# The last 20 rows of adj on four row groups of TensorE, one for each column block, in five products with adj

## The chip, the cores and the metric

The kernel runs on one core of a Trainium2 chip. The metric is device time in microseconds (us) for one execution; the time of a kernel is the median of several runs. One further execution was recorded by the hardware profiler, and all views of the profile are of that one.

Engines are named as in the profile: PE is TensorE's matmul stream and PEld its weight loads, DVE is VectorE, ACT is ScalarE, POOL is GpSimd, SP is the engine whose queue issues most DMAs. "L255" is line 255 of the kernel before.

## The reference, cut to what matters

Four graph layers on 2708 nodes with 128 features each. Every layer normalizes, and every layer multiplies by the same 2708x2708 matrix adj at least once:

```python
h = relu(layernorm(x))
x = x + L0(h, adj)     # z = leaky(d*(adj @ (d*h)) @ W1 + b1); S = exp(-dist(z)/2), top 4 a row
                       # d2*((S + adj) @ (d2*h)) @ W2 + b2
h = relu(layernorm(x))
x = x + L1(h, adj)     # attention: num = adj @ exp(leaky(r_i + c_j)); H = adj @ (att @ h W)
h = relu(layernorm(x))
x = x + L2(h, adj)     # h @ W_self + (adj @ h / deg) @ W_neigh
h = relu(layernorm(x))
x = x + L3(h, adj)     # relu(adj @ h @ K + b)
```

All data are float32. The products that this case is about are adj times a 2708x128 matrix: two in layer 0, and one each in layers 1, 2 and 3.

## The kernel before

adj is handed in transposed, as `adjT`. The 2708 rows of `adjT` are cut into T = 22 **chunks** of 128 rows; the last one (`i = T - 1 = 21`) has only TAIL = 20 rows. The 2708 columns are cut into six **column blocks** `KBS`: five of 512 and one of 148. The node dimension is also grouped by four chunks into six `GROUPS`, which coincide with the column blocks.

A product is made by `aggregate(y, done, more, kept)`. Its right-hand side `y` lies in SBUF as `[128, 22, 128]` (node in chunk, chunk, feature). For each column block `b` there is one PSUM bank `acc(b)`. `product(i, b)` is one float32 matmul: stationary `y[:w, i, :]`, moving `chunk(i)[:w, block b]`, summed into `out[b]` over all 22 chunks. In the profile each float32 matmul is two records on PE and two weight loads on PEld, under L255.

The loop over chunks has two parts:

- For `i` below `last`, chunk by chunk: all six blocks of chunk `i` are multiplied, while later chunks are loaded through the rotating pool `big` (4 buffers). After every second chunk one of the resident chunks is fetched.
- For `i` from `last` to 21 the chunks stay in SBUF under names `res17` to `res21` (5 of them, for the two products of layer 0) or `res16` to `res21` (6, for the three later products). This is the **tail**, and it goes block by block: for block `b` all remaining chunks, and then `done(b - 1, out)`, which takes the finished block before it out of PSUM and works on.

So in the tail the 20-row chunk comes once in each of the six blocks, as the last matmul of that block. The resident chunks are loaded once for the two products of layer 0 (in the earlier stage that sums the rows of adj on PE, L341), and once for the last three (during the product with `attended`).

The five products and what runs after each block:

| product | right side | `done` | made by |
|---|---|---|---|
| first | `y1` | `to_z` (L390) | `scale_nodes`, L372 |
| second | `y2` | `done_l0` (L653) | L498 to L505, ACT and DVE |
| third | `attended` | `to_h2` (L1181) | `attend` (L1154), called from `node_product` through `ahead` |
| fourth | `h2` | `to_h3` (L1204) | `layernorm_relu` in `to_h2` |
| fifth | `h3` | `to_out` (L1229) | `layernorm_relu` in `to_h3` |

In the second product there is also a stream of 88 indirect DMAs from POOL (L524, `add_near`), four for each chunk of nodes: each gathers rows of `y2` from its copy `ydr` in DRAM, and DVE adds them to `xs` (L530). Those for chunks 0 to 14 are emitted before the product, those for chunks 15 to 21 within `done_l0` and after it. They have 24 buffers.

A scheduler orders the instructions of an engine by the order of the program and by when it thinks they are ready. What is wrapped in `pin(...)` keeps its order among the pinned ones. All loads of chunks are pinned, on SP's queue. The matmuls of `aggregate` are not.

The lines that the change touches most:

Of the kernel before, what the change touches and what calls it, by code (L numbers as in the profile page):

```python
# [18 lines left out]
P = 128  # L19
# [6 lines left out]
def kernel(  # L26
# [18 lines left out]
    nc = tc.nc  # L45
    N, D = x.shape
    assert D == P
    T = -(-N // P)
    TAIL = N - (T - 1) * P
    KBS = [(k0, min(512, N - k0)) for k0 in range(0, N, 512)]  # L50
    NKB = len(KBS)
# [4 lines left out]
    def width(t):  # L56
        return TAIL if t == T - 1 else P
# [88 lines left out]
    def evacuate(dst, src):  # L146
        turn[0] ^= 1
        if turn[0]:
            nc.vector.tensor_copy(dst, src)
        else:  # L150
            nc.scalar.copy(dst, src)

    def pin(ins):

        return tc.keep_in_program_order(ins)

    def acc(b):
        return ps_a.tile([P, 512], F32, name=f"acc{b}")
# [4 lines left out]
    def layernorm_relu(dst, g):  # L163

        t0, t1 = GROUPS[g]
        n = t1 - t0
        st = small.tile([P, 4, 6], F32, name="ln_st")
        mv = small.tile([P, 4, 2], F32, name="ln_mv")
        rs = small.tile([P, 4], F32, name="ln_rs")
        for t in range(t0, t1):  # L170
            nc.vector.bn_stats(st[:, t - t0, :], xs[:, t, :])
            nc.vector.bn_aggr(mv[:, t - t0, :], st[:, t - t0, :])
        root = nc.scalar.activation(rs[:, :n], mv[:, :n, 1], AF.Sqrt, bias=ln_eps)
        nc.vector.reciprocal(rs[:, :n], rs[:, :n])
        nm = small.tile([P, 4], F32, name="ln_nm")
        nc.vector.scalar_tensor_tensor(
            nm[:, :n], mv[:, :n, 0], -1.0, rs[:, :n], op0=ALU.mult, op1=ALU.mult
        )
        for t in range(t0, t1):
            o = t - t0  # L180
            nc.scalar.activation(
                dst[:, t, :],
                xs[:, t, :],
                AF.Relu,
                scale=rs[:, o : o + 1],
                bias=nm[:, o : o + 1],
            )
        return root

    def scale_nodes(dst, src, v, t0, t1):  # L190
        nc.vector.tensor_tensor(
            dst[:, t0:t1, :],
            src[:, t0:t1, :],
            v[:, t0:t1, None].to_broadcast([P, t1 - t0, D]),
            ALU.mult,
        )
# [8 lines left out]
    def transposed(dst, src, g, copy=evacuate):  # L205

        t0, t1 = GROUPS[g]
        p = ps_s.tile([P, 512], F32, name="ps")
        for t in range(t0, t1):
            o = (t - t0) * P  # L210
            nc.tensor.transpose(
                p[:, o : o + width(t)], src[: width(t), t, :], ident[: width(t), : width(t)]
            )
        copy(dst[:, span(g)], p[:, : span(g).stop - span(g).start])

    def node_product(srcT, w, g, use, behind=False):

        t0, t1 = GROUPS[g]
        p = ps_s.tile([P, 4, P], F32, name="ps")
        for t in range(t0, t1):  # L220
            if w is None:
                nc.tensor.transpose(p[: width(t), t - t0, :], srcT[:, cols(t)], ident)  # L222
            else:
                mm = nc.tensor.matmul(  # L224
                    p[: width(t), t - t0, :], srcT[:, cols(t)], w, start=True, stop=True
                )
                if behind and t == t0:
                    pin(mm)
        for t in range(t0, t1):
            use(t, p[: width(t), t - t0, :])  # L230
# [4 lines left out]
    def chunk(i):  # L235
        if i in resident:
            return resident[i]
        if i >= T - pools["n"]:
            c = resident[i] = pools["res"].tile([P, N + 1], F32, name=f"res{i}")
        else:  # L240
            c = big.tile([P, N + 1], F32, name="chunk", tag="big")
        pin(nc.sync.dma_start(c[: width(i), :N], adjT[i * P : i * P + width(i), :]))
        return c

    def aggregate(y, done, more=None, kept=0):

        out = [acc(b) for b in range(NKB)]
        last = T - pools["n"]  # L250

        def product(i, b):
            k0, n = KBS[b]
            w = width(i)
            nc.tensor.matmul(  # L255
                out[b][:, :n],
                y[:w, i, :],
                chunk(i)[:w, k0 : k0 + n],
                start=(i == 0),
                stop=(i == T - 1),  # L260
            )

        for i in range(last):
            if more is not None:
                more(i)
            resident[i] = chunk(i)
            for b in range(NKB):
                product(i, b)
            if i < last - kept:
                del resident[i]  # L270
            if i % 2 and last + i // 2 < T:
                chunk(last + i // 2)
        if more is not None:
            for i in range(last, T):
                more(i)
        for b in range(NKB):
            for i in range(last, T):
                product(i, b)
            if b:
                done(b - 1, out)  # L280
        done(NKB - 1, out)

    NG = len(GROUPS)
# [14 lines left out]
    y1 = lay.tile([P, T, D], F32, name="y1", tag="Y")  # L298
# [35 lines left out]
    for i in range(T):  # L334
        c = chunk(i)
        w = width(i)
        if 3 <= i < 3 + 3 * NG:
            weighted((i - 3) // 3, i % 3)
        for b, (k0, n) in enumerate(KBS):
            g = 32 * (b % 4)  # L340
# [5 lines left out]
                stop=(i == T - 1),  # L346
            )
    sum_rows = lay.tile([P, 1024], F32, name="sum_rows", tag="U")
    for half, p0, p1 in ((0, 0, 128), (1, 0, 32 * (NKB - 5)), (1, 32 * (NKB - 5), 32 * (NKB - 4))):
        n = KBS[4 * half + p0 // 32][1]  # L350
# [3 lines left out]
    for b, (t0, t1) in enumerate(GROUPS):  # L354
        j = b % 4
        for t in range(t0, t1):
# [6 lines left out]
                stop=True,  # L363
# [7 lines left out]
    nc.gpsimd.tensor_tensor(xs, xs, b2[:, None, :].to_broadcast([P, T, D]), ALU.add)  # L371
    for t0, t1 in GROUPS:  # L372
        scale_nodes(y1, y1, dinv, t0, t1)
    uT = lay.tile([P, N], F32, name="u1T", tag="U")
    z = lay.tile([P, T, D], F32, name="z", tag="Z")
    zT = lay.tile([P, N], F32, name="zT", tag="T")
# [13 lines left out]
    def to_z(g, s1):  # L390
# [24 lines left out]
        evacuate(sq_rows[:, span(g)], p[:3, : span(g).stop - span(g).start])  # L415

    aggregate(y1, to_z)


# [23 lines left out]
    for t in range(T):  # L443
        w = width(t)
# [49 lines left out]
    y2 = lay.tile([P, T, D], F32, name="y2", tag="Y")  # L494
# [25 lines left out]
    def add_near(t, late=False):  # L520
        w = width(t)
        for k in range(TOPK):
            g = res.tile([P, D], F32, name="gath", bufs=24)
            nc.gpsimd.indirect_dma_start(  # L524
                out=g[:w, :],
                out_offset=None,
                in_=ydr[:, :],
                in_offset=bass.IndirectOffsetOnAxis(ap=near_u[:w, t, k : k + 1], axis=0),
            )
            term = nc.vector.scalar_tensor_tensor(  # L530
                xs[:w, t, :],
                g[:w, :],
                simd[:w, t, k : k + 1],
                xs[:w, t, :],
                op0=ALU.mult,
                op1=ALU.add,
            )
            if late and k == 0:
                pin(term)
# [127 lines left out]

    for t in range(15):
        add_near(t)
    aggregate(y2, done_l0, kept=4)  # L670
    transposed(hT, h1, NG - 2, nc.scalar.copy)
    column_terms(NG - 3)
    for t in range(GROUPS[-1][0], T):
# [295 lines left out]
    for t0, t1 in GROUPS:  # L969
        p = acc(1 + t0 // 4 % 5)  # L970
        for t in range(t0, t1):
# [6 lines left out]
                stop=True,  # L978
# [171 lines left out]
    attended = lay.tile([P, T, D], F32, name="attended", tag="Y")  # L1150
# [3 lines left out]
    def attend(t, p):  # L1154
        w = width(t)
        nc.vector.tensor_scalar(attended[:w, t, :], p, wk[:w, t : t + 1], None, op0=ALU.mult)

    def ahead(step, lead):


        def more(i):
            if i == 0:
                for g in range(min(lead + 1, NG)):
                    step(g)
            elif i % 4 == 0 and i // 4 + lead < NG:
                step(i // 4 + lead)

        return more
# [5 lines left out]
    h2 = lay.tile([P, T, D], F32, name="h2", tag="H")  # L1174
# [6 lines left out]
    def to_h2(g, s3):  # L1181
        k0, n = KBS[g]
        evacuate(u3T[:, k0 : k0 + n], s3[g][:, :n])
        node_product(u3T, None, g, add_x)
        layernorm_relu(h2, g)

    aggregate(attended, to_h2, ahead(lambda g: node_product(yT, None, g, attend), 1))

    def own(i):
# [6 lines left out]
    h3 = lay.tile([P, T, D], F32, name="h3", tag="Y")  # L1196
# [7 lines left out]
    def to_h3(g, s4):  # L1204
        k0, n = KBS[g]
        evacuate(u4T[:, k0 : k0 + n], s4[g][:, :n])
        node_product(u4T, wn, g, add_l2)
        layernorm_relu(h3, g)

    aggregate(h2, to_h3, own)  # L1210
    u5T = lay.tile([P, N], F32, name="u5T", tag="Z")

# [66 lines left out]
```

## Time and profile before

| | us |
|---|---|
| median of 3 runs | 1230.08 |
| lowest, highest | 1226.93, 1233.35 |
| the profiled execution's own time | 1316.51 |
| its span, first to last instruction | 1314.5 |
| PE busy (3637 matmul records) | 1094.3, 83% |
| DVE busy | 564.0, 43% |
| ACT busy | 408.5, 31% |
| POOL busy | 229.7, 17% |
| data moved by DMA | 297.31 MB, mean 226 GB/s |
| mean granted TensorE clock | 0.894 |

The five products lie, in us from the start of the span, at about 95 to 203, 350 to 545, 981 to 1086, 1086 to 1202 and 1202 to 1310. The profiled execution is 86 us longer than the median of the runs, so a stage of it has to be read with the clock that was granted in it (the row PEclk of the page, or the clock of a window).

In a group line the columns are: line, engine, operation, output<-inputs, partitions of the operands, shape, count | busy us, mean ns of one | idle time of the engine before them and what ended it. In a timeline line: start us, duration us, engine, line, operation, count, and in brackets the idle time before it and its releaser.

### The profile page before, as it was taken

What the parts mean: (1) busy time and instruction counts of PE and PEld (TensorE: products, weight loads), DVE (VectorE), ACT (ScalarE), POOL (GpSimd) and SP (SyncE); (2) the same over time, 40 slices, a digit from 0 to 9 for tenths busy, and PEclk for the clock granted to TensorE, in tenths of its full rate; (3) what the DMA queues carried; (4) which work ended last, traced back from release to release, by engine and by line L of the source; (5) the groups of instructions that cost most, each with busy time, mean ns of one, the idle gap of its engine ahead of it and who ended that gap; (6) DMA issues with size and microseconds to landing.
All of it is one profiled execution on the core that took longest, in us unless ns stands there. A gap on an engine that the chain in (4) does not pass through costs nothing.

```text
span 1314.5 us, 10207 instructions
## 1 busy us (share of the span) xinstructions
PE 1094.3 (83%) x3637; PEld 516.1 (39%) x3637; DVE 564.0 (43%) x1172; ACT 408.5 (31%) x643; POOL 229.7 (17%) x188
## 2 busy tenths in 40 slices
PE   4979999999673379897777771687899999999998
PEld 1334444444231134463433330233344445545444
DVE  2020026999722001782466564899960021113003
ACT  3100014444400001474566643677830021003000
POOL 1100000000077700034111103577400000000000
PEclk7989999999895569777899885798879999999999
DMA  8997700000562261255899998999939926752831
GB/s 316 425 383 268 282 0 1 1 0 0 193 245 95 94 249 55 86 241 227 227 395 376 359 374 328 422 425 423 351 127 417 354 81 224 268 185 80 302 125 43
DMA packets 39506, 297.31 MB, mean 226 GB/s; under 512 B 6749, under 2 KB 10680, under 8 KB 13116
## 3 DMA queue, kind: packets, MB, share of 16 engines
q1 hardware_dynamic: 23806, 201.04, 39.9%
q0 software_dynamic: 13216, 93.62, 18.9%
q10 hardware_dynamic: 2434, 2.01, 0.6%
q8 instruction: 29, 0.48, 0.1%
q14 instruction: 21, 0.17, 0.0%
HBM read 264.46 MB, written 32.87 MB: 226 GB/s over the span
## 4 chain that ended last, share of the span: by engine, by line
PE 57%; DMA 18%; DVE 11%; issue 10%; POOL 3%; ACT 1%; another core or an unknown queue 0%; SPq 0%; POOLq 0%; DVEq 0%; ACTq 0%
PE acc L255 37%; DMA mov<-in_adj_dram,src_u 8%; PE acc L448 8%; DVE hi L1116 4%; DVE hi L1104 4%; DMA chunk<-in_adj_dram 3%; DMA hi<-table,hi_u 2%; POOL gath L524 2%; PE acc L454 2%; DMA res<-in_adj_dram 2%; PE ps L341 1%; PE ps L224 1%; PE acc L1126 1%; DMA xs<-in_x_dram 1%; PE ps L222 1%
## 5 line engine op out<-in xcount | busy, mean ns | idle before, releaser
L255 PE MATMUL acc<-chunk,y 128*128 128x512 f32 (+1 forms) x408 | 178.8, 588 | 72.7 <-issue 60.1
L1126 PE MATMUL acc<-hi,xw 128*128 128x512 f32 (+2 forms) x264 | 120.9, 618 | 61.5 <-DVE hi L1116 61.5
L524 POOL DMA_INDIRECT gath<-ydr,near_u x88 | 83.4, 948 | 407.9 <-DMA ydr<-y 321.3
L255 PE MATMUL acc<-chunk,h 128*128 128x512 f32 (+1 forms) x384 | 148.0, 542 | 0.0
L255 PEld LDWEIGHTS acc<-chunk,y 128*128 128x128 f32 x408 | 79.0, 204 | 172.4 <-issue 160.6
L1021 PE MATMUL acc<-mov,wt 128*128 128x512 f32 (+1 forms) x264 | 115.2, 588 | 35.8 <-DMA mov<-in_adj_dram,src_u 35.7
L448 PE MATMUL acc<-zT 128*128 128x512 f32 (+2 forms) x264 | 107.7, 552 | 0.0
L1126 PEld LDWEIGHTS acc<-hi,xw 128*128 128x128 f32 (+1 forms) x264 | 54.3, 214 | 127.9 <-DVE hi L1116 64.6
L1025 DVE COPY mov<-acc 2x512 f32<-2x512 f32 (+1 forms) x126 | 74.3, 611 | 63.8 <-PE acc L1021 62.2
L255 PEld LDWEIGHTS acc<-chunk,h 128*128 128x128 f32 x384 | 68.8, 190 | 74.1 <-issue 74.1
L1021 PEld LDWEIGHTS acc<-mov,wt 128*128 128x128 f32 x264 | 51.0, 204 | 96.1 <-issue 69.9
L457 ACT COPY strip<-acc 128x512 f32<-128x512 f32 (+2 forms) x132 | 60.5, 557 | 71.4 <-issue 58.5
L255 PE MATMUL acc<-chunk,attended 128*128 128x512 f32 x192 | 73.5, 545 | 0.0
L448 PEld LDWEIGHTS acc<-zT 128*128 128x128 f32 (+1 forms) x264 | 46.6, 186 | 56.3 <-issue 35.5
L1026 ACT COPY knots<-acc 128x512 f32<-128x512 f32 x88 | 50.5, 586 | 57.4 <-DVE mov L1025 45.2
L1058 POOL DMA_INDIRECT lo<-table,lo_u x22 | 56.1, 2548 | 67.4 <-DVE hi L1104 31.6
L1104 DVE SCALAR_TENSOR_TENSOR hi<-lo,lam,hi 128x2708 f32<-128x2708 f32 (+4 forms) x25 | 67.2, 2697 | 1.0
L1116 DVE SCALAR_TENSOR_TENSOR hi<-row_all,inv_s,hi 128x2708 f32<-128x2708 f32 (+4 forms) x25 | 67.0, 2693 | 0.0
L1108 ACT ACTIVATE hi<-hi,lam 128x2708 f32<-128x2708 f32 (+4 forms) x25 | 56.7, 2280 | 32.3 <-issue 23.2
L459 DVE MAX8 top_v<-strip 128x8 f32<-128x2708 f32 (+1 forms) x22 | 64.7, 2966 | 0.5 <-ACT strip L457 0.4
L461 DVE FIND_INDEX8 top_i<-top_v,strip 128x8 uint32<-128x2708 f32 x20 | 59.2, 2973 | 0.0
L255 PE MATMUL acc<-res,h 128*128 128x512 f32 (+1 forms) x144 | 58.9, 551 | 0.0
(267 smaller groups left out, 1167.8 us busy)
## 6 DMA issues: line engine op xcount, KB each, us to landing
chunk<-in_adj_dram SPq DMA_DIRECT2D x110, 1354.0 KB
table<-knots SPq DMA_DIRECT2D x20, 1354.5 KB
res<-in_adj_dram SPq DMA_DIRECT2D x9, 1354.0 KB
ydr<-y SPq DMA_DIRECT2D x2, 704.0 KB
gath<-ydr,near_u POOLq DMA_INDIRECT x88
chunkY<-in_adj_dram SPq DMA_DIRECT2D x1, 1354.0 KB
chunkU<-in_adj_dram SPq DMA_DIRECT2D x1, 1354.0 KB
table<-knots SPq DMA_DIRECT2D x1, 1333.3 KB
```

The lines of the kernel that those rows point to most:

```text
L255: nc.tensor.matmul(out[b][:, :n], y[:w, i, :], chunk(i)[:w, k0 : k0 + n], start=(i == 0), stop=(i == T - 1),)
L448: mm = nc.tensor.matmul(zz[b][:w, :n], zT[:, cols(t)], zT[:, k0 : k0 + n], start=True, stop=False)
L457: nc.scalar.copy(s[:w, k0 : k0 + n], zz[b][:w, :n])
L459: nc.vector.max(top_v[:w, t, :], s[:w, :])
L461: nc.vector.max_index(top_i[:w, t, :], top_v[:w, t, :], s[:w, :])
L524: nc.gpsimd.indirect_dma_start(out=g[:w, :], out_offset=None, in_=ydr[:, :], in_offset=bass.IndirectOffsetOnAxis(ap=near_u[:w, t, k : k + ...
L1021: nc.tensor.matmul(p[:, :n], wt[:, t, :], moving[t][:, k0 : k0 + n], start=True, stop=True)
L1025: nc.vector.tensor_copy(moving[t + 1][:2, k0 : k0 + n], p[:2, :n])
L1104: nc.vector.scalar_tensor_tensor(num, lo[:w, c], kap, num, op0=ALU.mult, op1=ALU.add)
L1108: nc.scalar.activation(num, num, AF.Ln, scale=sc)
L1116: nc.vector.scalar_tensor_tensor(att[:w, c], row_all[:w, c], inv_s[:w, t : t + 1], att[:w, c], op0=ALU.max, op1=ALU.mult,)
L1126: nc.tensor.matmul(py[b][:, :n], xw[:w, t, :], att[:w, k0 : k0 + n], start=(t == 0), stop=(t == T - 1),)
```

## The change

Chunk 21 is loaded four times, to partitions 0, 32, 64 and 96. Likewise the 20 rows `y[:20, 21, :]` are copied by three small DMAs (`spread`) to partitions 32, 64 and 96, on SP's queue for `y2` and on POOL's for the other four. The six matmuls of chunk 21 use the row group `32 * (b % 4)`, and stand together, ahead of the other resident chunks instead of behind them in each block. The last chunk that closes a sum is now 20.

```diff
--- before.py
+++ after.py
@@ chunk
-        pin(nc.sync.dma_start(c[: width(i), :N], adjT[i * P : i * P + width(i), :]))
+        for g in range(4 if i == T - 1 else 1):
+            pin(
+                nc.sync.dma_start(
+                    c[32 * g : 32 * g + width(i), :N], adjT[i * P : i * P + width(i), :]
+                )
+            )
         return c
 
+    def spread(y, queue):
+
+        for g in range(1, 4):
+            queue.dma_start(y[32 * g : 32 * g + TAIL, T - 1, :], y[:TAIL, T - 1, :])
+
@@ aggregate
         def product(i, b):
             k0, n = KBS[b]
-            w = width(i)
+            r = slice(32 * (b % 4), 32 * (b % 4) + TAIL) if i == T - 1 else slice(0, P)
             nc.tensor.matmul(
                 out[b][:, :n],
-                y[:w, i, :],
-                chunk(i)[:w, k0 : k0 + n],
+                y[r, i, :],
+                chunk(i)[r, k0 : k0 + n],
                 start=(i == 0),
-                stop=(i == T - 1),
+                stop=(i == T - 2),
             )
...
         for b in range(NKB):
-            for i in range(last, T):
+            product(T - 1, b)
+        for b in range(NKB):
+            for i in range(last, T - 1):
                 product(i, b)
             if b:
                 done(b - 1, out)
@@ after scale_nodes of y1
+    spread(y1, nc.gpsimd)
@@
-    aggregate(y2, done_l0, kept=4)
+    aggregate(y2, done_l0, lambda i: spread(y2, nc.sync) if i == 4 else None, kept=4)
@@ attend
         nc.vector.tensor_scalar(attended[:w, t, :], p, wk[:w, t : t + 1], None, op0=ALU.mult)
+        if t == T - 1:
+            spread(attended, nc.gpsimd)
@@ to_h2
         layernorm_relu(h2, g)
+        if g == NG - 1:
+            spread(h2, nc.gpsimd)
@@ to_h3
         layernorm_relu(h3, g)
+        if g == NG - 1:
+            spread(h3, nc.gpsimd)
```

## The prediction

> **What bounds the kernel now.** I first asked for each engine's busy time in the stretches of the five products, since the page's shares mix stages.
>
> ```profile
> core 0: us, PE busy (x) PEld busy (x) DVE busy (x) ACT busy (x) POOL busy (x), PEclk, DMA share, GB/s
> 174.00:203.00 29.00, 29.00 (x101) 13.21 (x100) 12.02 (x38) 6.52 (x29) 0.00 (x0) 1.00 0.00 0
> 385.00:476.00 91.00, 31.29 (x36) 9.76 (x35) 14.37 (x41) 0.00 (x0) 59.19 (x63) 0.52 0.29 92
> 510.00:545.00 35.00, 34.87 (x125) 16.45 (x123) 18.79 (x83) 14.04 (x33) 3.62 (x4) 1.00 0.07 22
> 981.00:1054.00 73.00, 73.00 (x192) 34.35 (x192) 0.89 (x4) 0.00 (x0) 0.00 (x0) 0.99 0.97 389
> 1054.00:1086.00 32.00, 32.00 (x98) 14.51 (x97) 10.94 (x57) 8.57 (x19) 0.00 (x0) 1.00 0.14 53
> 1167.00:1202.00 35.00, 35.00 (x120) 17.22 (x118) 12.64 (x60) 7.58 (x19) 0.00 (x0) 1.00 0.13 49
> ```
>
> PE is busy all the time in the loops and in the tails (174 to 203, 510 to 545, 1054 to 1086, 1167 to 1202), and DVE at most 54% of a tail. So what leaves PE in a tail comes off the end, unless a chain behind it is close. One stretch is of another kind: from 385 to 476 the granted clock is 0.52 and PE does 36 records in 91 us. The second product's loop takes 350.2 to 510.0, 159.8 us; seventeen chunks at 4.54 us (below) are 77.2. **82.6 us of the profiled execution are this stretch**: 1316.5 - 82.6 = 1233.9, within the runs shown (1226.9 to 1233.4). I count gains against that and subtract them from the median.
>
> Next, what a 20-row matmul costs, from the weight loads around one in the third product's tail, in order of time:
>
> ```profile
> 1057.13 0.19 PEld L255 LDWEIGHTS acc<-res,attended 128*128 128x128 f32 x1 [0.24 <-issue]
> 1057.56 0.19 PEld L255 LDWEIGHTS acc<-res,attended 128*128 128x128 f32 x1 [0.24 <-issue]
> 1058.51 0.29 PEld L255 LDWEIGHTS acc<-res,attended 20*128 20x128 f32 x2 [0.76 <-issue]
> 1059.56 0.30 PEld L255 LDWEIGHTS acc<-res,attended 128*128 128x128 f32 x2 [0.76 <-issue]
> 1060.09 0.19 PEld L255 LDWEIGHTS acc<-res,attended 128*128 128x128 f32 x1 [0.24 <-issue]
> ```
>
> Among 128-row matmuls a load comes every 0.43 us, so a 512-column float32 matmul (two records) takes 0.858, the 148-column one 0.25, and a chunk 5 x 0.858 + 0.25 = 4.54. From the load at 1057.56 to that at 1060.09 there are five steps: 5 x 0.43 = 2.15, but 2.53 passed. The gaps of 0.76 say where: the first load of the 20-row matmul, and the first after it, were not made ahead; each waited for the matmul before it. **A visit to the 20-row form costs 0.39 us beside its 0.86.**
>
> Last, how PE runs matmuls on separate strips of the array. The row sums (L341) do, on four column strips; below it is one chunk there, and then one block of the fourth product's tail:
>
> ```profile
> 47.68 1.90 PE L341 MATMUL ps<-chunk,ones 128*32 128x512 f32 x12 [0.74 <-DMA chunk<-in_adj_dram]
> ...
> 1179.18 5.51 PE L255 MATMUL acc<-res,h 128*128 128x512 f32 x12
> ```
>
> Twelve records both, but 1.90 us against 5.51. Six float32 matmuls of the same widths went as two rounds: four strips side by side, then two.
>
> [...]
>
> **The change part by part.**
>
> Removed, in each product: six visits. Five of 512 columns: 0.858 + 0.39 = 1.25 each; where transposes or small matmuls follow instead of L255 the way out is 0.05 cheaper (starts of records), mostly so. The last: 0.25 + 0.39. Sum 5 x 1.25 + 0.64 - 0.25 = 6.6 us.
>
> Added, in each product: one visit with all six. Row group 0 does block 0 and then block 4: 1.72 us; group 1 does 1 and 5 within that. With one way in and out: 1.72 + 0.39 = 2.1. No row shows four row groups at 512 columns, so bounds: below, 2.0[...]; with no overlap 10 x 0.43 + 0.25 + 0.39 = 4.9. I take 2.1, since the strips of L341 came out as two full rounds. **Net 4.5 us a product, 22.5 for five.**
>
> Moved: chunk 21's matmuls go ahead of the tail, so its load and `y`'s last rows must be there some 25 us earlier. For `y1`, `h2`, `h3` the copies follow the last `layernorm_relu` or `scale_nodes`, 70 us or more ahead of the tail. For `attended`, `attend(21)` stands at i = 20 in the program's order, but all 22 L1156 are done at 981.9, before the loop. For `y2` the copies wait for `ydr`'s stores, done when POOL's gathers begin at 358. POOL copies: four products, three issues of about 1 us (the indirect ones take 0.95), landing some 2.4 us later as the gathers do; POOL is idle there, and nothing queues behind but what comes tens of us later. SP copies: three issues of 0.33 us, ahead of chunk loads that wait for buffers anyway. Nothing, as long as the scheduler keeps them early; if `attend(21)` fell to the tail, PE would wait about 6 us (transposes, DVE, issue, landing) once.
>
> Added loads: chunk 21 four times instead of once, twice in the kernel. Its load signals from 11 queues where full ones signal from 16[...]; full chunks land 3.24 us apart when queued, and I take four 20-row loads as one of these[...], 2.4 us more. SP issues six more, 0.35 us each. In the row-sum stage, which waits for DMA, the first copy alone is needed at 86.8 and the others come behind it; the first product's chunks, landing at 89.8, 93.0, 96.3 and 99.5, are due at 95.0 and every 4.54 us after: 2.4 us later still in time (the first by 2.8). In the third product the DMA share is 0.97. Completions in the trace show chunk 12, the one behind chunk 21, landing at 1031.8 and needed at 1035.4: a margin of 3.6 against 2.4. Nothing, up to 1 us.
>
> Who is late next? First product: the chain of `to_z` (DVE 3.5 us a block: the 12.0 above fall in the 20 us from 183, at 5.9 a block) against PE's new block of 4.7, with the steps taking turns on both: I take off 0.5. Second: the gathers. POOL issues one every 1.25 us from 358.0:
>
> ```profile
> 358.02 1.12 POOL L524 DMA_INDIRECT gath<-ydr,near_u  x1 [321.25 <-DMA ydr<-y]
> ...
> 462.15 0.94 POOL L524 DMA_INDIRECT gath<-ydr,near_u  x1 [0.30 <-issue]
> ```
>
> At full clock the tail would begin at 427, and DVE would use those for chunk 19 (the 80th lands at about 459.6) at 464.1 minus what is saved by then, 4: no margin left. I take off 1. Fourth and fifth: DVE has room, PE goes on at once (the fourth) or the last block's chain only shifts (the fifth).
>
> Sum: 22.5 - 0.5 - 1 = 21 us. 1230.1 - 21 = **1209 us**.
>
> **The rivals.**
>
> *The rows don't run side by side*, since the scheduler separates the six, or row groups are served in turn. Then a product saves 6.6 - 4.9 = 1.7: 8.5 us, 1221.5. For it: no row shows row groups at this width. Against: L341. With separate visits the gain falls to nothing.
>
> *The tails are not worth their PE time.* If the gathers hold the second product and `to_z` the first, three products remain, 13.5 us; less 1 for chunk 12: 1217. For it: the margin of 0 us and the short block above. Against: DVE is at 41% in the first tail.
>
> *Slower: the granted clock.* The stretch at 0.52 cost 82.6 us and sits within a product's loop, PE dense, DMA at 0.8 just before. If packed matmuls, or tails with fewer gaps, bring such a stretch into the timed runs, all falls at once: at half clock PE needs 1 us more for each us of work, so 21 us of matmul time in it make the gain zero, and a stretch like that seen gives 1209 + 83 = 1292. Against: nothing in the change raises the work in the loops, where it occurred.
>
> **How the numbers follow.** A measurement of this kernel tells about 0.5% (6 us) from no change. The forecast 0.67; tails not worth their time 0.15, still faster; rows in turn 0.08, of which 0.05 faster; no packing or an offsetting stall 0.04, same; clock 0.06, slower. Faster 0.87, same 0.07, slower 0.06. The range: below, 22.5 us from the fastest run shown (1226.9) is 1204, and 1 us for a cheaper visit: 1203. Above it takes in both faster rivals and their spread: 1223.
>
> **What would show it.** One group of 20-row matmuls ahead of each tail, its twelve records within about 2.1 us, two rounds with four starts close together; every block of the tails shorter by 1.2 us; third to fifth product each shorter by 4.5, with the strip stage (L448) starting 4 earlier after the first. Wrong: the twelve records 0.43 us apart; PE idle before the group, released by DMA of a copy; PE idle at chunk 12 of the third product; DVE's L530 released by `gath` in the second tail and the stage behind it no earlier.

## The result, and the profile after

| | before | after |
|---|---|---|
| median of 20 runs, us | 1231.11 (1226.34 to 1236.05) | 1220.99 (1213.77 to 1229.95) |
| ratio after to before | | 0.9929, 95% interval 0.9913 to 0.9946 |
| profiled execution's own time, span, us | 1316.51, 1314.5 | 1218.29, 1216.2 |

So the change is worth about 9 us (0.71% of 1231; the interval gives 6.6 to 10.7), where 21 were forecast. The group of six matmuls came out as predicted. Less than half of its worth reached the end.

The profile before had a long slow stretch in the second product (granted clock 0.52). For the comparison by stages I use a second profile of the kernel before, taken with the experiments, which has none (span 1228.2). A stage goes from the first matmul of `aggregate` in a product (or the first of the totals, L832) to the next such start, in us:

| stage | before | after | difference | predicted |
|---|---|---|---|---|
| start and row sums, to the first product | 96.2 | 97.6 | +1.4 | 0 |
| first product and strips, to the second | 255.9 | 255.3 | -0.6 | -4.0 |
| second product, to the totals | 138.1 | 133.7 | -4.4 | -3.5 |
| totals, table, attention, to the third | 404.0 | 401.4 | -2.6 | 0 |
| third product, to the fourth | 105.4 | 109.3 | +3.9 | -4.5 |
| fourth and fifth, to the last matmul of `aggregate` | 222.0 | 212.6 | -9.4 | -9.0 |
| the rest | 6.6 | 6.3 | -0.3 | 0 |

The fourth stage holds no edit. Over ten profiles of this study without the slow stretch it ran from 399.8 to 409.4, in no order that follows the edits, so its -2.6 says nothing. The two stages that stand out are the first and the third product.

First the windows over PE's parts of the products after, in answer to those of before (columns as there):

```profile
core 0: us, PE busy (x) PEld busy (x) DVE busy (x) ACT busy (x) POOL busy (x), PEclk, DMA share, GB/s
178.00:203.00 25.00, 25.00 (x96) 12.32 (x95) 10.04 (x30) 6.04 (x29) 0.00 (x0) 1.00 0.00 0
888.00:970.00 82.00, 76.88 (x194) 35.83 (x192) 1.19 (x5) 0.00 (x0) 1.62 (x3) 0.96 0.96 357
970.00:996.00 26.00, 26.00 (x85) 12.61 (x85) 9.33 (x47) 8.17 (x18) 0.00 (x0) 1.00 0.18 63
```

The loop of the third product (888 to 970) now has 5.1 us in which PE does nothing; before it had none. The first tail (178 to 203) still shows PE busy all the time, and yet nothing was gained there; that column misled me, as shown below.

The weight loads around the group of six, third product, in order of time:

```profile
969.68 0.19 PEld L267 LDWEIGHTS acc<-chunk,attended 128*128 128x128 f32 x1 [0.24 <-issue]
970.02 0.31 PEld L267 LDWEIGHTS acc<-res,attended 20*128 20x128 f32 x8 [0.15 <-issue]
970.55 0.19 PEld L267 LDWEIGHTS acc<-res,attended 20*128 20x128 f32 x2 [0.23 <-issue]
970.98 0.19 PEld L267 LDWEIGHTS acc<-res,attended 20*128 20x128 f32 x2 [0.24 <-issue]
971.93 0.30 PEld L267 LDWEIGHTS acc<-res,attended 128*128 128x128 f32 x2 [0.75 <-issue]
```

Twelve loads, of which eight go at once: two rounds, as forecast. From 970.02 to the first 128-row load at 971.93 it is 1.91 us. The step behind that is 0.53 in place of 0.43, and on PE the first 20-row matmul starts 0.22 behind the 148-column one ahead of it, in place of 0.13. So the visit costs 1.91 + 0.10 + 0.09 = 2.1, the forecast. In the first product the first four starts lie within 20 ns.

The third product in the timeline of PE:

```profile
888.04 51.98 PE L267 MATMUL acc<-chunk,attended 128*128 128x512 f32 x132
942.32 6.51 PE L267 MATMUL acc<-chunk,attended 128*128 128x512 f32 x12 [2.29 <-DMA chunk<-in_adj_dram]
951.65 18.44 PE L267 MATMUL acc<-chunk,attended 128*128 128x512 f32 x48 [2.83 <-DMA chunk<-in_adj_dram]
...
980.62 0.60 PE L222 MATMUL ps<-ident,u3T 128*128 128x128 f32 x4
981.05 4.46 PE L267 MATMUL acc<-res,attended 128*128 128x512 f32 x10
985.35 0.60 PE L222 MATMUL ps<-ident,u3T 128*128 128x128 f32 x4
```

The tail is right: a block takes 985.35 - 980.62 = 4.73 us, against 1071.03 - 1065.10 = 5.93 before:

```profile
1065.10 0.66 PE L222 MATMUL ps<-ident,u3T 128*128 128x128 f32 x4
...
1071.03 0.66 PE L222 MATMUL ps<-ident,u3T 128*128 128x128 f32 x4
```

But chunk 11 comes 2.29 us late and chunk 12 another 2.83, and the 12 records between them take 6.51 us, where the 48 behind them take 18.44: the mean clock granted between 938 and 956 is 0.91. The chunk that was late first had been issued *ahead* of the four loads of chunk 21. What moved meanwhile, in the DMA view of 932 to 948, 40 slices of 0.4 us (first row: busy tenths of the 16 engines):

```profile
DMA  9999959969997959979979979896979998999999
GB/s 433 433 433 433 379 108 190 217 135 217 217 217 135 271 81 162 162 108 163 162 108 135 163 108 163 163 190 190 325 271 406 406 406 298 433 379 406 379 406 379
```

For some 10 us the engines stay almost as busy as before and move 81 to 271 GB/s in place of 406 to 433. The busy share hides it; the second row shows it.

### The profile page after: what moved, and what is told of

It is laid out like the page before. It is cut to its first block, busy times and chain, and to the rows that moved or that the text cites. A ratio compares the mean times of both kernels' runs of the same rounds, so it can differ in the third digit from the quotient of the medians.

```text
span 1216.2 us, 10253 instructions
## 1 busy us (share of the span) xinstructions
PE 1054.7 (87%) x3637; PEld 507.0 (42%) x3637; DVE 563.8 (46%) x1172; ACT 407.5 (34%) x643; POOL 237.0 (19%) x200
## 4 chain that ended last, share of the span: by engine, by line
PE 53%; DVE 20%; DMA 19%; issue 6%; POOL 1%; ACT 1%; SPq 0%; POOLq 0%; DVEq 0%; ACTq 0%
PE acc L267 40%; DMA mov<-in_adj_dram,src_u 7%; DVE top_v L474 5%; DMA chunk<-in_adj_dram 5%; DVE top_i L476 5%; DVE hi L1131 4%; DVE hi L1119 4%; DMA hi<-table,hi_u 2%; DMA res<-in_adj_dram 2%; PE ps L847 2%; PE acc L1036 2%; PE acc L1141 1%; PE ps L224 1%; DMA xs<-in_x_dram 1%; PE ps L355 1%
## 5 line engine op out<-in xcount | busy, mean ns | idle before, releaser
L267 PE MATMUL acc<-chunk,y 128*128 128x512 f32 (+1 forms) x408 | 159.3, 554 | 12.8 <-DVE y L518 10.7
L267 PE MATMUL acc<-chunk,h 128*128 128x512 f32 (+1 forms) x384 | 148.0, 542 | 0.0
L1036 PE MATMUL acc<-mov,wt 128*128 128x512 f32 (+1 forms) x264 | 119.7, 608 | 28.7 <-DMA mov<-in_adj_dram,src_u 28.7
L267 PEld LDWEIGHTS acc<-chunk,y 128*128 128x128 f32 x408 | 75.0, 194 | 97.1 <-issue 85.6
L463 PE MATMUL acc<-zT 128*128 128x512 f32 (+2 forms) x264 | 108.2, 552 | 1.5 <-ACT strip L472 1.1
L267 PEld LDWEIGHTS acc<-chunk,h 128*128 128x128 f32 x384 | 68.8, 190 | 74.1 <-issue 74.1
L267 PE MATMUL acc<-chunk,attended 128*128 128x512 f32 x192 | 76.9, 563 | 5.1 <-DMA chunk<-in_adj_dram 5.1
L463 PEld LDWEIGHTS acc<-zT 128*128 128x128 f32 (+1 forms) x264 | 46.4, 185 | 57.3 <-issue 34.1
L545 DVE SCALAR_TENSOR_TENSOR xs<-gath,simd,xs 128x128 f32<-128x128 f32 (+1 forms) x88 | 30.6, 351 | 59.9 <-DMA gath<-ydr,near_u 59.2
```

Source lines behind the costliest of these rows:

```text
L267: nc.tensor.matmul(out[b][:, :n], y[r, i, :], chunk(i)[r, k0 : k0 + n], start=(i == 0), stop=(i == T - 2),)
L463: mm = nc.tensor.matmul(zz[b][:w, :n], zT[:, cols(t)], zT[:, k0 : k0 + n], start=True, stop=False)
L1036: nc.tensor.matmul(p[:, :n], wt[:, t, :], moving[t][:, k0 : k0 + n], start=True, stop=True)
```

## The experiments

Each is timed beside the kernel before on one chip; 95% intervals in brackets.

**The kernel before again** (no edit).

> The kernel before, once more, for a profile in which no long stretch is throttled. Theory (the five tails gain unequally): its second product's loop runs at full clock in about 77 us, the first tail's blocks take about 6.2 us each by the chain of to_z as in the profile already shown, the third product takes 103.8 us, the fourth and fifth together 221.7 us. Rival (the stages differ from profile to profile by several us whatever the kernel): these move by more than 1.5 us.

Span 1228.2, one run at 1230.2 us. Its stages are the "before" column above: loop of the second product without the slow stretch, the third 105.4 by this table's ends, fourth and fifth 222.0. Between the two profiles of before the first product with the strips repeats within 0.7 us (255.2 and 255.9) and the third product within 0.3 (105.1 and 105.4).

**Copies of chunk 21 loaded later.**

```diff
-        for g in range(4 if i == T - 1 else 1): (four loads)
+        (one load in chunk(); the other three in copies())
@@ aggregate, loop over chunks
             resident[i] = chunk(i)
+            if i == late:
+                copies()
-    aggregate(y1, to_z)
+    aggregate(y1, to_z, late=8)
(and late=15 in the third product)
```

> The changed kernel with the three extra copies of chunk 21 loaded later: in the first product after chunk 8's load, in the third after chunk 15's. The work of all engines is the same. Theory (the four 20-row loads hold up the chunks that are queued beside them): the third product loses its waits for chunks 11 and 12 and takes 99.3 us in place of 108.3; the row-sum stage ends up to 2.5 us earlier; the whole about 10 us less than the changed kernel, 1210 us, a ratio to before of 0.983. Rival (the third product's waits have another cause, DMA being at its limit there anyway): as the changed kernel, 1221 us, 0.992.

1213.91 us, ratio 0.9872 (0.9825 to 0.9920), 7 us below the change's 1220.99. PE's wait in the third product is gone:

```profile
L271 PE MATMUL acc<-chunk,attended 128*128 128x512 f32 x192 | 73.7, 546 | 0.0
```

That stage takes 102.2, not the 109.3 of the change: 7.1 us less, where 9 were expected. The rival falls. Against the kernel before the stage gains 3.2 and so lacks 1.3 of the 4.5 of the prediction, and PE's order tells why: one of the six 20-row matmuls stands behind block 0, apart from the others, and paid for a visit of its own (0.39 + 0.86).

**The loads alone**, in the kernel before.

```diff
-        pin(nc.sync.dma_start(c[: width(i), :N], ...))
+        for g in range(4 if i == T - 1 else 1):
+            pin(nc.sync.dma_start(c[32 * g : 32 * g + width(i), :N], ...))
```

> The kernel before with only the three extra copies of chunk 21 loaded, at the change's places in the queue; no matmul reads them and the tails are the old ones. Theory (these loads hold up the chunks beside them): the third product takes about 9 us more, with PE waiting for chunks 11 and 12, and the row-sum stage up to 2.5 us more: 1240 us, 1.007. Rival (the loads cost what their bytes cost, at most 2.4 us, with a margin of 3.6): 1231 us, 1.000.

1236.19 us against 1230.67, ratio 1.0050 (1.0029 to 1.0070). The loads alone cost 5.5 us by the medians. PE waits 2.41 us for a chunk in the third product, which takes 108.4 (+3.0, not 9); the row sums end at 98.2 (+2.0). The direction is the theory's, the third product's share is smaller than in the change.

**One load of 60 rows instead of three of 20**, in the kernel before: the same bytes.

```diff
+        if i == T - 1:
+            pin(nc.sync.dma_start(c[32:92, :N], adjT[N - 60 : N, :]))
```

> The kernel before with one more load at the change's places in the queue: the last 60 rows of adj into partitions 32 to 91 of chunk 21's tile, in one transfer, read by nobody. These are the bytes of the change's three extra copies, on 15 queues in place of 10. Theory[...]: the extra load passes in about 1.5 us, PE doesn't wait in the third product, which stays within 1 us of 105.4, and the row sums end at most 1 us later: 1231.5 us, 1.001. Rival (the bytes cost, with DMA at its limit in both stages): as with the three copies, 1236 us, 1.0045.

1231.02 us against 1228.76, ratio 1.0011 (0.9991 to 1.0031); third product 105.3, row sums done at 95.5. So the bytes are innocent. The DMA view of 940 to 956, to be set beside that of the change:

```profile
DMA  9999997699789999999899999999999999999999
GB/s 433 433 433 406 217 217 163 162 298 298 190 325 433 433 406 433 433 433 406 379 433 433 433 433 433 433 433 433 433 406 406 379 379 406 406 406 406 433 433 406
```

The dip lasts some 3 us in place of 10. It can be put in numbers by the completions of the full chunks that stand ahead of and behind the small loads (11 and 12); queued full chunks land 3.24 us apart, and what exceeds that is the price of the small loads between them. In the third product: one 20-row load 0.9 us (the kernel before; 0.0 to 1.5 over five profiles); with the 60-row one 2.1; with three more of 20 rows 6.7 (loads alone) and 6.1 (the change).

**Three loads of 40 rows by half the columns**, in the kernel before: again the same bytes.

```diff
+            for p0, c0 in ((32, 0), (32, half), (72, 0)):
+                pin(nc.sync.dma_start(
+                    c[p0 : p0 + 40, c0 : c0 + half], adjT[N - 40 : N, c0 : c0 + half]))
```

> The kernel before with three extra loads at the change's places in the queue, of 40 rows by half the columns each: the bytes, the count of transfers and the 10 queues of the change's three extra copies, but twice the partitions[...]. Read by nobody. Theory[...]: these pass in about half the time of the 20-row ones, the third product loses at most 1 us of the 3.0 that those cost it, and the row sums under 1: 1231.5 us, 1.001. Rival[...]: as with the three 20-row copies, third product 3 us longer, 1234 to 1236 us, 1.0045.

1319.87 us against 1317.96, ratio 1.0017 (0.9998 to 1.0037). On this run's chip every execution, of every kernel, ran some 86 us longer, and its profiles have a slow stretch in the second product, as the first profile before has; only differences on that chip are used. The theory's 1.001 lies in the interval, the rival's 1.0045 outside. In the profile PE waits 1.22 us for a chunk in the third product, which takes 106.7 (105.1 and 105.4 before, 108.4 with the 20-row loads). The landings lie between the two: the small loads between the two full chunks cost 5.3 us, not much less than four of 20 rows (6.7 and 6.1) and far more than with the 60-row load (2.1). So the time speaks for the theory, by which loads over twice the partitions take half the time, and the landings more for the rival, by which loads with as many landing signals and transfers as those of 20 rows cost what those do; the cause stays open. The expected half was my own estimate, from the count of partitions; no run had shown it.

**Later in the first product alone.**

```diff
-    aggregate(attended, to_h2, ahead(...), late=15)
+    aggregate(attended, to_h2, ahead(...))   (three loads again right behind chunk 21's first)
```

> The changed kernel with the extra copies of chunk 21 later in the first product alone (after its chunk 8); in the third they stand where the change has them. Theory (most of the 7 us that the later loads brought come from the third product): the third product still waits for chunks 11 and 12 and takes 108 to 109 us; 5 us slower than with both later, 1218.9 us, 0.991. Rival (the row sums hold most of it): the third product's loss is 2 us or less, 1215.5 us, 0.988.

1305.68 us on the same chip as the run before, ratio 0.9909 (0.9886 to 0.9933), 12.3 us below before: the theory's 0.991 lies in the interval, the rival's 0.988 just outside. The profile says more:

```profile
1035.00 20.14 PE L273 MATMUL acc<-chunk,attended 128*128 128x512 f32 x48 [3.35 <-DMA chunk<-in_adj_dram]
```

PE waits for chunk 12 alone, not for 11, and the 48 records behind take 20.14 us in place of 18.44, at a granted clock of 0.50 between 1036.0 and 1039.4. The third product takes 106.4, 4.2 more than with later loads. It is the change's third product once more, with the same edit, and 2.9 shorter than in the change's own profile.

**The group in the fourth and fifth product alone.**

```diff
-    aggregate(y1, to_z)   aggregate(y2, ...)   aggregate(attended, ...)
+    (these three with packed=False; copies() in the fourth product, late=4)
```

> The four row groups in the fourth and fifth product alone; the first three as before; the extra copies of chunk 21 are loaded once, in the fourth product after its chunk 4. Theory (these two gain 4.7 each, the first gains nothing, the third loses 4.5 and the row sums 2.5, the second is small): 9.4 us less than before, 1221.5 us, 0.9924, the same as the whole change. Rival (the first and second product gain too, 3 us or more each, and something else takes it back): this kernel is still at 1221.5, but moving the copies in the whole change then gives more than 10 us.

1220.27 us against 1230.67, ratio 0.9921 (0.9896 to 0.9945), the same as the whole change. The two products take 213.3 in place of 222.0. The three others together had given nothing that these times show.

**The group in the first and second product alone**, copies loaded after chunk 8.

```diff
-    aggregate(attended, ...)   aggregate(h2, to_h3, own)   aggregate(h3, to_out)
+    (these three with packed=False; late=8 in the first)
```

> The four row groups in the first and second product alone, with the copies of chunk 21 loaded after the first product's chunk 8; the last three products as before. Theory (the first gains 0.5 and 1.1 in the strips, the second 2 to 4.4, as the profiles show): 5 us less than before, 1225.7 us, 0.996. Rival (the prediction's steps: first 4, second 3.5): 7.5 us less, 1223.2 us, 0.994.

1226.22 us against 1228.76, ratio 0.9979 (0.9963 to 0.9994): 2.5 us less, between 0.7 and 4.5. The rival's 7.5 is excluded, and the theory's 5 too, only just. The profile has 1.1 from the first stage and 2.1 from the second product.

**to_z's steps one block apart**, in the kernel before. `to_z(g)` is cut behind `z`; what follows (norms, `zT`, `parts`) runs for block g - 1.

```diff
         nc.vector.scalar_tensor_tensor(zv, zv, 0.1, zv, op0=ALU.mult, op1=ALU.max)
+        if g:
+            norms(g - 1)
+        if g == NG - 1:
+            norms(g)
+
+    def norms(g):
+        t0, t1 = GROUPS[g]
         for t in range(t0, t1):
```

> The kernel before with the steps of to_z taken one block apart: the transposes of block g and its z come before the norms, zT and parts of block g - 1, so that PE's L222 of a block no longer stands behind L412 of the block before it. Theory (the first tail's blocks are set by to_z's chain at 6.3 us, with PE's own 5.9 close behind): the first MAX8 comes up to 1.5 us earlier after the product's start, 1229.5 us, 0.999. Rival (PE sets the tail): no difference, 1230.7 us.

1229.38 us against 1228.76, ratio 0.9994 (0.9977 to 1.0011): no difference that can be measured. In the profile the first product with the strips takes 254.8 in place of 255.9; the first MAX8 comes 120.7 us after the product's start in place of 127.0, more than I had thought, but it is the end of the stage that counts.

**The same cut, with the group of six and later loads.**

> The changed kernel with the copies of chunk 21 loaded later (as in the run with later loads) and, besides, the steps of to_z taken one block apart. Theory (in the first tail the chain of to_z took PE's place as the bound, which is why packing gained nothing there): the blocks fall from 6.3 us to about 4.9, the first MAX8 comes 4 to 5 us earlier after the product's start than the 126.6 of the run with later loads, and the whole is 4.4 us less: 1209.5 us, 0.983. Rival (something else holds the first tail, the evacuations or DVE's work): as the run with later loads, 1213.9 us, 0.987.

1208.68 us against 1228.76, ratio 0.9828 (0.9795 to 0.9862), 20 us below before. The first product with the strips takes 250.7, against 254.6 with later loads alone: the same cut that gave 1.1 us of this stage in the kernel before, and no time that could be measured, gives 3.9 here. The first MAX8 is at 116.5 after the start, 10 earlier, where 4 to 5 were expected; part of that is given back in the strips. PE's timeline in that tail:

```profile
191.95 0.60 PE L222 MATMUL ps<-ident,u1T 128*128 128x128 f32 x4
...
196.67 0.66 PE L222 MATMUL ps<-ident,u1T 128*128 128x128 f32 x4
...
201.55 0.60 PE L222 MATMUL ps<-ident,u1T 128*128 128x128 f32 x4
...
204.70 0.66 PE L222 MATMUL ps<-ident,u1T 128*128 128x128 f32 x4
```

L222 starts a block's `to_z`. It comes every 4.7, 4.9 and 3.2 us here, 4.1 in the mean of the five steps. In the change it comes every 6.3 us (five steps):

```profile
186.70 0.60 PE L222 MATMUL ps<-ident,u1T 128*128 128x128 f32 x4
...
217.98 0.44 PE L222 MATMUL ps<-ident,u1T 128*128 128x128 f32 x2
```

And so it did before the change, in the first profile:

```profile
183.08 0.66 PE L222 MATMUL ps<-ident,u1T 128*128 128x128 f32 x4
...
214.66 0.44 PE L222 MATMUL ps<-ident,u1T 128*128 128x128 f32 x2
```

**All of that, and the group behind block 0's other matmuls** in place of ahead of them.

```diff
-        for b in range(NKB):
-            product(T - 1, b)
         for b in range(NKB):
             for i in range(last, T - 1):
                 product(i, b)
+            if b == 0:
+                for k in range(NKB):
+                    product(T - 1, k)
```

> Later loads and to_z's steps one block apart, as in the run before with both, and besides chunk 21's group of six behind block 0's other matmuls in place of ahead of them. In the run with later loads one of the third product's six 20-row matmuls stood alone behind block 0, at 0.39 us and 0.86 more, since its copy was expected late; here all six stand there together. Theory (that stray visit is what the third product lacks of its 4.5): third product 101 us in place of 102.2, the whole 1.2 us less, 1207.5 us, 0.982. Rival (it costs nothing, or block 0's later evacuation takes it back in the other tails): 1208.7 us, 0.983.

1300.92 us on the chip with the slow stretch (before 1317.96), ratio 0.9870 (0.9847 to 0.9892): 17 us. The third product takes 100.6, so the stray visit was what it lacked. The total is some 4 us short of the expectation. The same kernel on another chip:

> The kernel with later loads, to_z's steps one block apart and chunk 21's group behind block 0, once more: in the run before, every execution of every kernel had the throttled stretch of some 85 us in the second product. Theory (its parts add up: first product 4.5 less than before, second 2 to 4, third 4.5, fourth and fifth 9.3): without that stretch 20.5 to 22 us less than before, 0.983. Rival (17 us, as measured with the stretch, is what it gives): 0.986.

1205.58 us against 1229.91, ratio 0.9820 (0.9789 to 0.9851). The rival's 0.986 lies just outside. This version beats both kernels. The interval is wide, 18 to 26 us, and holds the expected 20.5 to 22. By stages, against before: first product 250.4 (-5.5), second 135.9 (-2.2), third 100.5 (-4.9), fourth and fifth 212.6 (-9.4).

## Why the prediction was right and wrong

**The price of a 20-row visit and of the group: right.** 2.1 us for six, as forecast, two rounds, a block shorter by 1.2 (4.73 us against 5.93). The 2.1 us include the way in and out. That four row groups run as one full round I had only from the column strips of L341 (twelve records in 1.90 us). Here the first round of four took 0.96 us (970.02 to 970.98), against 0.858 for one 512-column matmul among the 128-row ones.

**Fourth and fifth product: right.** -9.4 against -9.0, and alone they make the whole change's time.

**Third product: the step that failed.** I wrote that four 20-row loads are as one full chunk, 2.4 us more, that chunk 12, "the one behind chunk 21", had a margin of 3.6, and "Nothing, up to 1 us". It lost 3.9 us where 4.5 were to be gained, 8.4 us in all; in the run with later copies in the first product alone, which has the same third product, it fell 5.5 short. What failed is the size of that term: between chunks 11 and 12 the four small loads cost 6.7 us with the loads alone, 6.1 in the change and 5.8 in that run, where I had taken 3.24 for all four. That is past the margin of 3.6, and PE waited 2.41, 2.83 and 3.35 us for chunk 12. Behind its waits the clock was granted at 0.50 for 3.4 us in two of the three profiles (from 942.9 in the change, from 1036.0 in that run), which cost 1.7 more: the 48 records of that run took 20.14 us in place of 18.44. The late wait fell where the prediction's last part had named it as a sign of error ("PE idle at chunk 12").

The change's own profile has one thing more: I had counted only what stands behind the small loads, but there chunk 11, ahead of them, landed 8.8 us behind chunk 10. Fifteen of its sixteen signals had come by 937.69; the last came at 942.27, later than nine of the ten landing signals of each of the first three small loads (by 937.29, 939.45 and 942.00). Why this one part was late isn't shown. In the two other profiles with four loads in a row chunk 11 landed 4.5 and 5.8 us behind chunk 10, and in five with one load 4.2 to 5.5.

*Why* such loads are dear isn't settled. The four landed 1.8, 1.4 and 1.5 us apart in the change, at 81 to 271 GB/s. Beyond the 0.9 of one 20-row load the landings give 4.4 us for the three loads of 40 rows, 4.9 to 5.8 for three of 20 rows and 1.2 for the 60-row one: the loads of 40 rows lie near those of 20 and not at the half that I had estimated. In the traces a load of 20 or 40 rows signals once half a microsecond after its issue and ten times as it lands, the 60-row one once and fifteen times; a full chunk signals sixteen times as it lands. (The prediction's 11 queues are these signals: one at the issue, ten at the landing.) By the count of landing signals alone 40 rows would cost what 20 do; they cost a little less. The runs differ in the count of transfers too, so neither the partitions nor the landing signals nor that count is shown to be the cause.

**First product: the second step that failed.** "I take off 0.5" for the chain of `to_z`; it took 3.4 of the 4.0 that were left (about 2.6 in the run with later loads). The rival *the tails are not worth their PE time* was right here. I had argued from PE busy for all 29.00 us of the tail and from DVE at 41%. Neither excludes a chain. Nor did I measure the blocks: I took 5.9 us a block, PE's own work, where the first profile's L222 already came every 6.3. Here is one block after the change, a short one of 5.7 us, from the timeline of all engines:

```profile
193.14 0.65 PE L222 MATMUL ps<-ident,u1T 128*128 128x128 f32 x4
...
193.85 1.11 DVE L401 SCALAR_TENSOR_TENSOR z<-ps,dinv,b 128x128 f32<-128x128 f32 x4
194.99 0.69 DVE L411 SCALAR_TENSOR_TENSOR z<-z 128x512 f32<-128x512 f32 x1
...
196.03 0.31 ACT L414 ACTIVATE junk<-z 128x128 f32<-128x128 f32 x1
...
197.45 0.16 DVE L418 TENSOR_SCALAR parts<-sq 128x4 bf16<-128x4 f32 x1
...
198.25 0.17 DVE L422 CAST parts<-rest 128x4 bf16<-128x4 f32 x1
198.48 0.39 PE L427 MATMUL ps<-ident_b,parts 128*3 128x128 bf16 x4
198.80 0.66 PE L222 MATMUL ps<-ident,u1T 128*128 128x128 f32 x4
```

Each line waits for the one above (ACT 0.35 us longer, behind an evacuation of its own), and the next block's L222 stands on PE behind this block's L427: PE, DVE, ACT, DVE, PE, one after the other, with DVE and ACT less than half full (10.04 and 6.04 of 25 us). PE's own work for a block is 8 x 0.43 of L267, 0.44 for each of the two transposes and 0.34 for L427: 4.7 us after, 5.9 before with the visit. The chain's 6.3 was above both. PE looked full before since it spread its matmuls into the chain's gaps; after, it had done them by 201.3 and went on with the strips (L463), whose first MAX8 still needs the last block. From 255.9 the stage fell to 254.8 by the cut alone, to 254.6 by the group with later loads alone, and to 250.7 by both.

**Second product: the sign right, the size open.** Forecast 3.5. The change's own profile has 4.4, the four others without the slow stretch 2.1 to 2.2. PE's part ends 3.7 to 5.1 earlier, the last of the 88 gathers is issued 117 to 118 us after the product's start in all of them, and behind it `done_l0` has a chain like that of `to_z`. Which of the two keeps the rest was not tried.

**Row sums: "the first copy alone is needed", nothing.** In the change they end 1.4 us later, with the loads alone 2.0. The first part holds: PE doesn't wait for a copy. But it waits for the last resident chunks, and behind such waits the clock was at half in five profiles (last section), three of them without extra loads in this stage; the copies are at most one cause among others.

**The granted clock** stayed out of the result: the slower rival did not come. In the timed runs the slow stretch goes with a chip, not with a kernel: on one, all 19 runs of before took 1310 to 1324 us and the 26 of the three kernels beside it 1295 to 1324; on the three others of the experiments none did. Taking it off the profiled execution before counting gains was right, though 1233.9 is not within the runs shown but 0.5 above the highest. And "the granted clock" is not the whole of it: in the prediction's own line PE is busy for 31.29 of the 91 us, with 36 records, where at half of the 0.43 us pace it would do 91 / 0.86, about 106. In the other 60 us PE was idle, and the page names no releaser for that ("issue 60.1"). What held it there is open.

In sum: of 21 us, the third product took 8.4 (5.5 in the second profile of it) and the first 3.4. With both mended, 20 and 24 us were measured, and 17 on the chip with the slow stretch.

## What to carry to other kernels

A busy engine in a tail is not yet its bound: look for the step of each block that starts only when the block before has gone all the way round the engines, and measure its pitch (6.3 us here, against 4.7 of PE's own work); cutting that chain (1.1 us of the stage) and shortening the engine's work (1.3) paid in full only together (5.2). A small load among the queued chunks of the third product (DMA share 0.96) was not priced by its bytes: place it where a full buffer's slack lies behind it (the third product took 102.2 us in place of 109.3), or load more rows at once (60 rows cost 1.2 us where three times 20 cost 5 to 6), and read GB/s beside the busy share (0.93 at 302 GB/s from 938 to 956 us in the change, 1.00 at 394 GB/s just before). If work on few rows is gathered into one group, put the group where its last operand is surely there: with later loads the scheduler took one of six apart, the visit was paid twice, and the third product took 102.2 us where the whole group took 100.6.

## What the runs showed of the hardware that I had not expected

At the end of the row sums PE waits for the chunk before the last and then has 24 matmuls. This took either 3.73 us or 5.15 to 6.51. Here is a slow one, in the kernel before with `to_z` cut, which has no extra load at all:

```profile
86.40 6.51 PE L341 MATMUL ps<-res,ones 128*32 128x512 f32 x24 [2.17 <-DMA res<-in_adj_dram]
92.84 5.83 PE L358 MATMUL acc<-ones,sum_rows 1*128 1x1 f32 x44
100.84 1.19 PE L255 MATMUL acc<-chunk,y 128*128 128x512 f32 x1 [2.17 <-DVE y L191]
```

After waits of 1.38 to 1.99 us it was 3.73 or two times 1.90 in every profile (eight of them); after 2.16 to 2.77 it was slow in five, and fast in one, the first profile of before (2.21). The clock tells the two apart. In the profile above it was granted at 0.78 from 86 to 88 us and at 0.50 from 88 to 94; in the first profile of before at 1.00 until 90. It fell to half before the first product in all fourteen profiles, but at 85.6 to 87.1 us in the slow ones, within the wait or the 24 matmuls, and at 88.6 to 92.6 in the fast ones, behind them. The first product then starts at 94.5 to 96.2 us or at 97.6 to 100.8. So half a microsecond of waiting more went with up to 5 us; that the wait brings on the fall is likely by these counts but was not tried. In the first profile of before the fall lasted 6.8 us (from 91.2), in the change 3.4 us (from 86.2) and then 10.2 (from 93.0).
